# A four-block transformer on one core: query and key stripes filled straight from the rotated tiles, and the opening reordered around ten hand-placed score steps

## The chip, the cores and the metric

The kernel runs on one core of a Trainium2 chip. The metric is the device time of one execution in microseconds (us). The engines meant below are TensorE (PE, matmul; PEld its weight loads), VectorE (DVE), ScalarE (ACT), GpSimd (POOL) and SyncE (SP, which here only issues DMAs). All data are float32.

## The reference, cut to what matters

Eight sequences of 512 tokens by 256 channels pass through four residual blocks. The first block is the attention that the change is about; the other three are the same for both kernels.

```python
x = x + attn_a(layernorm(x))        # 16 heads of 16, keys and values through a latent of 64, rotary q and k
x = x + ffn(layernorm(x))           # 256 -> 1024, relu, -> 256
x = x + attn_b(layernorm(x))        # retention: (q k^T * decay) v, one head of 256
x = x + ffn(layernorm(x))

# attn_a, per sequence and head
q = x @ Wq + bq
k, v = split((x @ Wkv_down + bkv_down) @ Wkv_up + bkv_up)
q, k = rope(q), rope(k)             # [x1 cos - x2 sin, x1 sin + x2 cos]
att = softmax(q k^T / 4 + log_sparse + log(decay + 1e-9))
out = att @ v + 0.2 * sigmoid(q . mean(k)) * mean(v)
return out @ Wo + bo
```

## The kernel before, in words

**Layout.** For each sequence b (a "batch" below) the 16 heads are four groups g of four heads; a head owns 32 partitions of the tiles `qT` and `kT` ([128, 4 groups, 512]), two of each, used in turn by even and odd batches. Of a head's 32 rows, 16 hold the rotated projection, one holds minus the row maximum (in qT) against a one (in kT), and the rest are zero in qT. So one matmul over 32 rows gives scores already shifted by their maximum.

**Opening of a batch.** A layer norm (`ln_units`: statistics on DVE, `rstd` on GpSimd, `norm` on DVE, `turn` = four transposes on PE and a copy on ACT, each in two halves of the tokens), `latent` (the down projection), then `projected(j, e)`: j is 0 for queries and 1 for keys, e is the half (dimensions 0 to 7 or 8 to 15 of all 16 heads), so that the result is [128 = 16 heads x 8, 512]. `half_unit` multiplies it by the cosine and the sine table (DVE, tiles `rc` and `rs`). `turn(j)` combines the halves on GpSimd, writes them to the DRAM tensors `dk` or `dq` (two moves) and reads them back into the 32-row layout of `kT` or `qT` (four moves, one for each head of a group). `mean_k`, `gate`, `mean_v` and `through_wo` make the small memory term.

**Score steps.** A batch has 32 steps, eight to a group: four query tiles by two pairs of heads. Step t does `score_item` (s: two matmuls into PSUM), `reduce_item` (DVE, the row maximum `mr`), and for step t-10 (LAG) `prob_item` (t: the transposed, shifted scores), `soft_item` (exponential on ACT; the product with the decay table on DVE or GpSimd), and for every second step `pv_item` two steps later (PVLAG). When a group's eight maxima are there, `shift` transposes them, negates them on ACT and sends them by a DMA that ACT issues (`neg`) into the row of qT.

**Order of the work.** Every engine runs its instructions in the order in which the program writes them (`keep_in_program_order`). All moves by `move` go through SyncE's queue in that order. For the opening the order is written by hand at the end of `tile_kernel`. After that a planner takes over: it holds chains of units (`Unit`: a function, its PE time, the engines it then needs, the units before it, the first step at which it may come), and at each turn either does the next score step or takes the unit that can start first. Fillers that use PE are paid from a credit that grows with each step by the PE work left, divided by the steps left. In the kernel before, the planner's loop starts at step 0; batch 0 is then fully projected, its values, gate and the product of the retention's weights (`plain`, `product`, `product_biases`) are done, and the fillers for the first steps are batch 0's `through_wo` (from step 10) and batch 1's layer norm (from step 2) and projections.

**Names in the profile.** Line 69 is the helper that records every DVE, ACT and GpSimd operation, 205 and 208 those for matmuls and transposes, 91 that for moves; so the tile names tell operations apart: `tr_a`, `lat`, `k`, `q`, `v`, `ga`, `mv`, `me` for the opening's units, `wr`, `ct`, `bb` for plain, product and product_biases, `s` and `t` for scores, `p` for probabilities, `hx` and `x` for the two halves of the feed-forward.

Of the kernel before, what the change touches and what calls it, by code (L numbers as in the profile page):

```python
# [35 lines left out]
def tile_kernel(  # L36
# [44 lines left out]
    dr = ctx.enter_context(tc.tile_pool(name="dr", bufs=1, space=bass.MemoryType.DRAM))  # L81
# [56 lines left out]

    qT = [keep([P, NG, T], f"qT{i}") for i in range(2)]
# [7 lines left out]
    dq = [dr.tile([NH, HD, T], F32, tag=f"dq{i}", name=f"dq{i}") for i in range(2)]  # L147
    dk = [dr.tile([NH, HD, T], F32, tag=f"dk{i}", name=f"dk{i}") for i in range(2)]
# [11 lines left out]
    def buffers(i, eng):  # L160
        eng.memset(kT[i], 1.0)
        eng.memset(qT[i], 0.0)
        gps.memset(vaug[i], 1.0)

    def head_mask():
        dve.reduce_sum(hmask, ident.rearrange("p (h d) -> p h d", d=HH), axis=AX.X)
        gps.tensor_scalar(hmask, hmask, 0.5 / T, None, ALU.mult)
        gps.memset(kmean, 0.0)

    def memory_buffers():  # L170
        for i in range(2):
            gps.memset(gates[i], 0.0)
            move(gates[i][NH : NH + 1, :], rope[HD : HD + 1, 0, :])
            gps.memset(mem[i], 0.0)
        gps.memset(bo_row, 0.0)
        move(bo_row[NH : NH + 1, :], rows[D : 2 * D].unsqueeze(0))
        move(bvc, rows[0:D].rearrange("(c p) -> p c", p=P))
        gps.memset(vmean, 0.0)
        gps.memset(vmask, 0.0)
        gps.memset(vmask[:, :, NH : NH + 1], 1.0)  # L180
        for c in range(NC):
            dve.reduce_sum(
                vmask[:, c, c * HH : (c + 1) * HH], ident.rearrange("p (h d) -> p h d", d=HD), axis=AX.X
            )
        gps.tensor_scalar(bvc, bvc, 0.1, None, ALU.mult)

    late = {}

    def late_loads():
        late["dec_a"] = resident(decay_a, "dec_a")  # L190
        xs[1] = load_x(1)

        for g in range(NG):
            at_row = (g % 2) * 4 * HD
            move(wo_sb[at_row : at_row + 4 * HD, g // 2, :], wo.rearrange("(h d) g n -> h d g n", d=32)[:, :HD, g, :])
        late["w1"] = resident(w1, "w1_sb")
        late["w2"] = resident(w2, "w2_sb")

        move(wvu[:, :, :D], wb[:, :, 2, :])
        late["dec_b"] = resident(decay_b, "dec_b")  # L200
# [12 lines left out]

    wq_sb = keep([P, NC, 2, P], "wq_sb")

    wk_sb = keep([P, P], "wk_sb")
    def regroup():
        for e in range(2):
            half_of = slice(e * HH, (e + 1) * HH)
            act.copy(  # L220
                wk_sb[e * LAT : (e + 1) * LAT, :].rearrange("p (h d) -> p h d", d=HH),
                wk_in[e * LAT : (e + 1) * LAT, :, half_of],
            )
        for e in range(2):
            half_of = slice(e * HH, (e + 1) * HH)
            for c in range(NC):
                act.copy(wq_sb[:, c, e, :].rearrange("p (h d) -> p h d", d=HH), wq_in[:, c, :, half_of])
# [4 lines left out]
    def biases():  # L232
        pick = keep([P, 2, 32], "pick")
        for e in range(2):
            act.copy(
                pick[:, e, :].rearrange("p (s d) -> p s d", d=HH),
                ident.rearrange("p (s d) -> p s d", d=32)[:, :, e * HH : (e + 1) * HH],
            )
        ps = misc("qk_bias")
        for g in range(NG):  # L240
            for j, v in enumerate((V_BQ, V_BK)):
                for e in range(2):
                    mm(ps[g * 32 : g * 32 + 32, 2 * j + e : 2 * j + e + 1], pick[:, e, :], vec[:, v + g : v + g + 1])
        act.copy(qk_bias.rearrange("p j e -> p (j e)"), ps[:, :4])
# [12 lines left out]

    def plain(j):
        ps = misc(f"wr{j}")
        for o in range(NC):  # L260
            for c in range(NC):
                flip(ps[:, o * D + c * P : o * D + (c + 1) * P], wqk_in[:, c, j, o * P : (o + 1) * P])
        wr[j] = rs.tile([P, NC, D], F32, tag="xr", bufs=3, name=f"wr{j}")
        act.copy(wr[j].rearrange("p o d -> p (o d)"), ps)

    def product():
        ps = misc("ct")
        for c in range(NC):
            for o in range(NC):
                mm(ps[:, c * D : (c + 1) * D], wr[1][:, o, c * P : (c + 1) * P], wr[0][:, o, :], o == 0, o == NC - 1)  # L270
        dve.tensor_copy(ct.rearrange("p c d -> p (c d)"), ps)
# [76 lines left out]
    def front1(b):  # L348
        def latent():
            ps = misc(f"lat_{b}")  # L350
            for c in range(NC):
                mm(ps, wd_sb[:, c].rearrange("p j n -> p (j n)"), xT_a[b]["xT"][:, c, :], c == 0, c == NC - 1)
            lt = fr.tile([P, T], F32, tag="lat", name=f"lat_{b}")
            lsum[b] = fr.tile([P, 1], F32, tag="lsum", name=f"lsum_{b}")
            act.activation(lt, ps, AF.Identity, bias=vec[:, V_BD : V_BD + 1], accum_out=lsum[b])
            lat_a[b] = lt
# [19 lines left out]
        def mean_v():  # L376
            ps = misc(f"mv_{b}")
            for c in range(NC):
                mm(ps[:, c : c + 1], wv_sb[:LAT, c * P : (c + 1) * P], lsum[b][:LAT])
            m = fr.tile([P, NC], F32, tag="mv_a", name=f"mv_a_{b}")  # L380
            dve.scalar_tensor_tensor(m, ps[:, :NC], 0.1 / T, bvc, ALU.mult, ALU.add)
            for c in range(NC):
                gps.tensor_scalar(vmean[:, c, : NH + 1], vmask[:, c, :], m[:, c : c + 1], None, ALU.mult)
# [9 lines left out]
        u = {"lat": Unit(latent, 1720, (("ACT", 700),), after=[h0[2], h1[2]])}  # L393
# [8 lines left out]
    def front2(b, u1):  # L402
        rot = {}
# [17 lines left out]
        def half_unit(j, e, ps):  # L421
            for n, table in (("c", cos), ("s", nsin)):
                t = fr.tile([P, T], F32, tag="rot", bufs=6, name=f"r{n}{j}{e}_{b}")
                dve.scalar_tensor_tensor(t, ps, qk_bias[:, j, e : e + 1], table, ALU.add, ALU.mult)
                rot[n, e] = t

        def turn(j):

            d = (dq, dk)[j][b % 2]
            for e in range(2):  # L430
                o = rot["c", e]
                if e == 0:
                    gps.tensor_add(o, o, rot["s", 1])
                else:
                    gps.tensor_sub(o, o, rot["s", 0])
                move(d[:, e * HH : (e + 1) * HH, :], o)
            src = d.rearrange("(g s) r t -> s r g t", s=4)
            to = (qT, kT)[j][b % 2]
            for h in range(4):
                move(to[h * 32 : h * 32 + HD], src[h])  # L440
            if j == 0:
                if b > 1:
                    move(to[HD:P:32], zero_rows)
                rot["q"] = rot["c", 0], rot["c", 1]

        def mean_k():
            m = fr.tile([P, 2], F32, tag="mk", name=f"mk_{b}")
            for e in range(2):
                unused = fr.tile([P, T], F32, tag="unused", name=f"unused{e}_{b}")
                act.activation(unused, rot["c", e], AF.Identity, accum_out=m[:, e : e + 1])  # L450
                gps.tensor_scalar(kmean[:, e, :NH], hmask, m[:, e : e + 1], None, ALU.mult)

        def gate():
            ps = misc(f"ga_{b}")
            for e in range(2):
                mm(ps, kmean[:, e, :], rot["q"][e], e == 0, e == 1)
            act.activation(gates[b % 2][:NH, :], ps[:NH, :], AF.Tanh)
# [9 lines left out]
        ga = Unit(gate, 1720, (("ACT", 600),), after=[km, qt], needs=(("wo", b - 2),))  # L467
        return [lat] + k + [kt, km] + q + [qt, u1["v"], ga, u1["mv"], u1["me"]]
# [23 lines left out]
    def shift(i):  # L492
# [5 lines left out]
        act.dma_start(qT[b % 2][HD:P:32, g, :], neg)  # L498
# [237 lines left out]
    order0 = front2(0, front[0][1])  # L736
    (n0, n1), u0 = (front[0][0][:3], front[0][0][3:]), front[0][1]
    buffers(0, dve)
    head_mask()
    n0[0].fn(), n1[0].fn()  # L740
    biases()
    regroup()
    n0[1].fn(), n1[1].fn()
    n0[2].fn(), n1[2].fn()
    memory_buffers()
    for u in order0[:7]:
        u.fn()
    late_loads()
    plain(0), plain(1)
    for u in order0[7:10]:  # L750
        u.fn()
    product(), product_biases()
    buffers(1, gps)


# [127 lines left out]
    for u in front[0][0] + order0[:10]:  # L883
        u.done = 0
    order0[10].step = 10
    chains = [order0[10:], setup]
    for b in range(1, B):
        ln0, u1 = front1(b)
        ln0[0].step = ln0[3].step = max(0, PER * (b - 1) + 2)
# [8 lines left out]
    t, credit, share = 0, 0, 0  # L898
# [156 lines left out]
```

## Time and profile before

| | us |
|---|---|
| median of 3 timed runs | 1343.89 (1341.66 to 1344.90) |
| profiled run, its time | 1341.52 |
| profiled run, span of the core | 1339.7 |
| TensorE busy | 1256.3 (94%) |
| VectorE busy | 811.0 (61%) |
| ScalarE busy | 450.0 (34%) |
| GpSimd busy | 405.8 (30%) |
| mean granted TensorE clock | 0.978 |

Times inside the profile count from the start of the span. A line of the timeline gives the start, the duration, the engine, the line, the operation, what it writes and reads, the shapes and the count of merged instructions; in brackets stands the idle time before it and what ended that. In a row of the stages, each engine has its busy time and its number of instructions, then come the granted TensorE clock as a share of full speed, the mean busy share of the 16 DMA engines and what they moved. Where the clock has no record, as in the first 20 us, the row shows 1.00; the durations of the matmuls tell there how fast the array ran. A float32 matmul appears as two instructions.

### The profile page before, as it was taken

Reading aid. Unit: us, or ns where it says so; the run is one execution under the profiler, and the core shown is the slowest. Engines: PE = TensorE matmul, PEld = TensorE weight load, DVE = VectorE, ACT = ScalarE, POOL = GpSimd, SP = SyncE. Lnnn points to the kernel's source line nnn. Section 1 sums busy time; section 2 is a strip of 40 time slices with the busy share of each in tenths; the row PEclk is TensorE's granted clock in tenths of the full one; section 3 lists DMA queues with packets and bytes.
Section 4 is the critical chain, followed back from the end, with each engine's and each line's share of the span. In section 5 each row is a group of like instructions: output and inputs, shape, how many; then the busy total and the mean of one; then the engine's idle time right before and its main releaser. Section 6 shows DMA issues by size and latency. Waiting matters only on the chain. (4 is left out here: it accounts for less than half of the span.)

```text
span 1339.7 us, 15533 instructions
## 1 busy us (share of the span) xinstructions
PE 1256.3 (94%) x6116; PEld 623.3 (47%) x6116; DVE 811.0 (61%) x1323; ACT 450.0 (34%) x646; POOL 405.8 (30%) x461
## 2 busy tenths in 40 slices
PE   6899888999899999999999999999999899999988
PEld 3333232534354455453443554544444445455665
DVE  4588885667656774657856666657755575343130
ACT  2044434333434334433334334333333333321201
POOL 4165542324412432215332323214321232222010
PEclk9599999989899999999999999999999999998999
DMA  5440030012000210004000310003000000000000
GB/s 133 133 80 1 1 80 1 1 26 55 1 17 1 62 19 1 1 17 80 1 1 1 74 22 1 1 9 73 1 1 5 12 1 1 1 17 1 0 16 16
DMA packets 22798, 32.34 MB, mean 24 GB/s; under 512 B 3627, under 2 KB 13228, under 8 KB 22446
## 3 DMA queue, kind: packets, MB, share of 16 engines
q1 hardware_dynamic: 22086, 31.10, 10.1%
q8 instruction: 48, 0.79, 0.3%
q10 hardware_dynamic: 640, 0.26, 0.1%
q14 instruction: 24, 0.20, 0.1%
HBM read 18.50 MB, written 12.58 MB: 23 GB/s over the span
## 5 line engine op out<-in xcount | busy, mean ns | idle before, releaser
L69 DVE TENSOR_REDUCE mr<-s 128x2 f32<-128x1024 f32 x256 | 312.8, 1222 | 251.7 <-PE t L205 237.2
L69 ACT ACTIVATE p<-t 128x1024 f32<-128x1024 f32 (+1 forms) x290 | 263.8, 924 | 519.3 <-PE t L205 476.3
L69 POOL TENSOR_TENSOR p<-p,dec_a 128x512 f32<-128x512 f32 x182 | 233.1, 1301 | 507.6 <-ACT p L69 495.0
L205 PE MATMUL s<-kT,qT 32*128 32x512 f32 x1024 | 295.3, 660 | 49.3 <-DVE mr L69 44.4
L205 PE MATMUL t<-qT,kT 32*128 32x512 f32 x1024 | 294.7, 642 | 0.3 <-ACT p L69 0.3
L69 DVE TENSOR_TENSOR p<-p,dec_a 128x512 f32<-128x512 f32 x330 | 228.9, 735 | 21.0 <-ACT p L69 20.8
L205 PE MATMUL x<-w_sb,h_x 128*128 128x256 f32 x1024 | 233.9, 384 | 0.0
L205 PEld LDWEIGHTS x<-w_sb,h_x 128*128 128x128 f32 x1024 | 190.8, 190 | 54.5 <-issue 30.1
L205 PEld LDWEIGHTS s<-kT,qT 32*128 32x128 f32 x1024 | 81.2, 189 | 221.8 <-DVE mr L69 97.5
L205 PE MATMUL pv<-p,va 128*32 128x512 f32 x1024 | 151.7, 612 | 2.9 <-DVE p L69 2.4
L69 ACT ACTIVATE h_x<-hx,vec 128x512 f32<-128x512 f32 x128 | 88.0, 687 | 151.8 <-PE hx L205 151.8
L205 PE MATMUL hx<-xT_f,w_sb 128*128 128x512 f32 x256 | 120.2, 609 | 0.7 <-ACT xT_f L69 0.7
L205 PE MATMUL hx<-xT_g,w_sb 128*128 128x512 f32 x256 | 119.3, 609 | 0.7 <-ACT xT_g L69 0.7
L69 DVE TENSOR_TENSOR x<-x,x 128x256 f32<-128x256 f32 x64 | 27.1, 423 | 148.3 <-PE x L205 148.3
L205 PEld LDWEIGHTS t<-qT,kT 32*128 32x128 f32 x1024 | 80.5, 184 | 15.9 <-ACT p L69 7.8
L205 PEld LDWEIGHTS hx<-xT_g,w_sb 128*128 128x128 f32 x256 | 46.8, 193 | 63.5 <-issue 58.1
L205 PEld LDWEIGHTS hx<-xT_f,w_sb 128*128 128x128 f32 x256 | 46.5, 194 | 58.3 <-issue 51.6
L205 PEld LDWEIGHTS pv<-p,va 128*32 128x32 f32 x1024 | 23.3, 108 | 79.3 <-issue 37.0
L69 POOL TENSOR_TENSOR x<-x,row 128x256 f32<-128x256 f32 x64 | 48.0, 770 | 32.1 <-DVE xn_f L69 21.4
L69 POOL TENSOR_TENSOR rc<-rc,rs 128x512 f32<-128x512 f32 x32 | 42.3, 1342 | 5.6 <-DVE rs L69 5.6
L205 PE MATMUL bs<-xT_r,ret 128*128 128x512 f32 (+3 forms) x128 | 38.0, 442 | 0.0
L205 PE MATMUL bo<-ret 128*128 128x256 f32 x160 | 36.6, 383 | 0.0
(130 smaller groups left out, 1020.1 us busy)
## 6 DMA issues: line engine op xcount, KB each, us to landing
dk<-rc SPq DMA_DIRECT2D x16, 256.0 KB, 2.9
kT<-dk SPq DMA_DIRECT2D x32, 128.0 KB, 3.2
dq<-rc SPq DMA_DIRECT2D x16, 256.0 KB, 2.9
qT<-dq SPq DMA_DIRECT2D x32, 128.0 KB, 3.8
out_dram<-x SPq DMA_DIRECT2D x32, 128.0 KB, 1.7
x<-in_x_dram SPq DMA_DIRECT2D x7, 512.0 KB, 3.6
w_sb<-in_w_dram SPq DMA_DIRECT2D x2, 1024.0 KB, 10.1
x<-in_x_dram SPq DMA_DIRECT2D x2, 256.0 KB
```

The costliest lines, as they stand in the source:

```text
L69: ins = f(*a, **k)
L205: tc.keep_in_program_order(nc.tensor.matmul(o, lhsT=l, rhs=r, start=start, stop=stop))
```

## The change

The DRAM tensors `dq` and `dk` are gone. A rotated tile goes to qT or kT by four moves, one for each group, each from 32 neighbouring partitions (four heads by eight dimensions) to 32 partitions that lie four apart (`stripes`). A head's row order changes with it (dimension d of half e lies at row 4d + 2e, the maximum at row 1), for queries and keys alike. So a turn is eight moves in place of six.

The opening is rewritten by hand: PE first runs 14 products of the identity (`warm`); batch 0's latent is computed in two halves, each as soon as its half of the tokens is transposed; queries' first half comes before the keys; the second query half is rotated on DVE in place of GpSimd; loads that the first steps need (second x, decay table, gate rows) are issued before the stripes, and the rest after them; memsets move from DVE to GpSimd or later on DVE. The first ten score steps are then called by hand, with `plain(1)`, the two halves of `product`, the shift of group 0 and batch 0's gate between them. Batch 0's `mean_v` (from step 12), `through_wo` and `product_biases` (from step 20) become fillers, and batch 1's layer norm may start from step 10 on. The planner starts at step 10, with no credit.

```diff
-    dr = ctx.enter_context(tc.tile_pool(name="dr", bufs=1, space=bass.MemoryType.DRAM))
...
+    def loads_before_scores():
+        xs[1] = load_x(1)
+        late["dec_a"] = resident(decay_a, "dec_a")
+        for i in range(2):
+            move(gates[i][NH : NH + 1, :], rope[HD : HD + 1, 0, :])
+        move(bvc, rows[0:D].rearrange("(c p) -> p c", p=P))
...
+    def warm(n):
+        ps = misc("warm")
+        for j in range(n):
+            mm(ps[:, j % 4 * P : (j % 4 + 1) * P], ident, ident)
...
-        def latent():
-            ps = misc(f"lat_{b}")
+        def latent(part=0, parts=1):
...
+            ps = misc(f"lat_{b}_{part}")
+            n = T // parts
+            cols = slice(part * n, (part + 1) * n)
...
+        def rotate(j, e, eng):
+            o = rot["c", j, e]
+            if e == 0:
+                eng.tensor_add(o, o, rot["s", j, 1])
+            else:
+                eng.tensor_sub(o, o, rot["s", j, 0])
+            rot[j, e] = o
+
+        def stripes(j, g, e):
+            move((qT, kT)[j][b % 2][2 * e : P : 4, g, :], rot[j, e][g * 32 : g * 32 + 32, :])
 
         def turn(j):
-
-            d = (dq, dk)[j][b % 2]
             for e in range(2):
-                o = rot["c", e]
-                if e == 0:
-                    gps.tensor_add(o, o, rot["s", 1])
-                else:
-                    gps.tensor_sub(o, o, rot["s", 0])
-                move(d[:, e * HH : (e + 1) * HH, :], o)
-            src = d.rearrange("(g s) r t -> s r g t", s=4)
-            to = (qT, kT)[j][b % 2]
-            for h in range(4):
-                move(to[h * 32 : h * 32 + HD], src[h])
-            if j == 0:
-                if b > 1:
-                    move(to[HD:P:32], zero_rows)
-                rot["q"] = rot["c", 0], rot["c", 1]
+                rotate(j, e, gps)
+                for g in range(NG):
+                    stripes(j, g, e)
+            if j == 0 and b > 1:
+                move(qT[b % 2][1:P:32], zero_rows)
...
-        act.dma_start(qT[b % 2][HD:P:32, g, :], neg)
+        act.dma_start(qT[b % 2][1:P:32, g, :], neg)
...
-    buffers(0, dve)
-    head_mask()
+    dve.memset(kT[0], 1.0)
+    gps.memset(vaug[0], 1.0)
+    memory_buffers()
+    picks()
+    warm(14)
+    regroup_k()
     n0[0].fn(), n1[0].fn()
+    n0[1].fn(), n1[1].fn()
+    n0[2].fn()
     biases()
-    regroup()
-    n0[1].fn(), n1[1].fn()
-    n0[2].fn(), n1[2].fn()
-    memory_buffers()
-    for u in order0[:7]:
-        u.fn()
+    regroup_q(0)
+    latent(0, 2)
+    masks()
+    dve.memset(qT[0], 0.0)
+    gps.memset(kT[1], 1.0)
+    gps.memset(qT[1], 0.0)
+    gps.memset(vaug[1], 1.0)
+    loads_before_scores()
+    n1[2].fn()
+    latent(1, 2)
+    regroup_q(1)
+    half_unit(0, 0, projected(0, 0))
+    k_ps = [projected(1, e) for e in range(2)]
+    half_unit(1, 0, k_ps[0]), half_unit(1, 1, k_ps[1], "sc")
+    rotate(1, 0, gps), rotate(1, 1, gps)
+    half_unit(0, 1, projected(0, 1), "sc")
+    rotate(0, 1, dve), rotate(0, 0, dve)
+
+    for g in range(NG):
+        for j, e in ((1, 0), (1, 1), (0, 1), (0, 0)):
+            stripes(j, g, e)
     late_loads()
-    plain(0), plain(1)
-    for u in order0[7:10]:
-        u.fn()
-    product(), product_biases()
-    buffers(1, gps)
+    order0[1].fn()
+    plain(0)
+    gps.tensor_scalar(bvc, bvc, 0.1, None, ALU.mult)
+    order0[0].fn()
...
+    ga0.after = []
+    mv0.step = 12
+    chains = [[mv0, me0, Unit(product_biases, 2400, (("DVE", 500),), step=20)], setup]
     for b in range(1, B):
         ln0, u1 = front1(b)
-        ln0[0].step = ln0[3].step = max(0, PER * (b - 1) + 2)
+        ln0[0].step = ln0[3].step = max(LAG, PER * (b - 1) + 2)
...
+    between = {
+        1: Unit(lambda: plain(1), 700, (("ACT", 600),)),
+        3: Unit(lambda: product(0), 900),
+        5: Unit(lambda: product(1), 900, (("ACT", 600),)),
+        9: ga0,
+    }
+    for t in range(LAG):
+        step(t)
+        if t in between:
+            issue(between[t])
+        if t == 8:
+            issue(posts.pop(0))
+
+    t, credit, share = LAG, 0, 0
```

In this cut `order0[1]` is batch 0's `values` and `order0[0]` its `mean_k`. A helper `spare` gives the second query half of batch 0 a tile of the probabilities' pool, the plain weights `wr` lie in the tile of `x1`, and the product's copy out of PSUM moves from DVE to ACT.

## The prediction

> **What bounds the kernel now.** I read the page first (busy times and the forty slices), then a table of stages, then the opening in order of time, then the steps after it, and last SyncE's waits and the DMA issues. The page:
>
> ```profile
> span 1339.7 us, 15533 instructions
> PE 1256.3 (94%) x6116; PEld 623.3 (47%) x6116; DVE 811.0 (61%) x1323; ACT 450.0 (34%) x646; POOL 405.8 (30%) x461
> PE   6899888999899999999999999999999899999988
> PEclk9599999989899999999999999999999999998999
> ```
>
> TensorE is the bound from the fourth slice on, and the change leaves that long part as it is: after the opening both kernels have the same matmuls to do. What can be won lies in the first two slices, where PE is at 6 and then "busy" at half clock. The stages of that opening:
>
> ```profile
> core 0: us, PE busy (x) PEld busy (x) DVE busy (x) ACT busy (x) POOL busy (x), PEclk, DMA share, GB/s
> 33.40:38.00 4.60, 0.00 (x0) 0.00 (x1) 1.48 (x2) 0.00 (x0) 1.49 (x2) 0.54 0.53 96
> 38.00:52.00 14.00, 13.96 (x29) 4.66 (x30) 8.71 (x13) 0.00 (x0) 0.95 (x2) 0.50 0.96 277
> 52.00:64.00 12.00, 10.35 (x33) 4.76 (x33) 6.69 (x11) 1.44 (x3) 0.95 (x2) 0.62 0.03 12
> 64.00:100.00 36.00, 33.07 (x166) 11.57 (x165) 29.15 (x35) 15.29 (x31) 21.37 (x19) 1.00 0.38 73
> 100.00:127.00 27.00, 26.99 (x155) 8.91 (x148) 21.43 (x28) 13.67 (x27) 16.03 (x13) 1.00 0.01 2
> ```
>
> For 4.6 us PE has nothing; then ten score steps run at clock 0.50. The timeline says what PE waited for:
>
> ```profile
> 11.88 3.78 PE L205 MATMUL lat<-xT_a,wd_sb 128*128 128x512 f32 x4 [0.92 <-ACT xT_a L69]
> 16.53 2.08 PE L205 MATMUL k<-lat,wk_sb 64*128 64x512 f32 x4 [0.87 <-ACT lat L69]
> 22.75 1.79 SPq L91 DMA_DIRECT2D dk<-rc  x2
> 27.07 1.74 SPq L91 DMA_DIRECT2D kT<-dk  x4
> 28.91 2.52 SPq L91 DMA_DIRECT2D dq<-rc  x2
> 34.74 1.72 SPq L91 DMA_DIRECT2D qT<-dq  x4
> 38.00 13.91 PE L205 MATMUL s<-kT,qT 32*128 32x512 f32 x28 [4.64 <-DMA qT<-dq]
> 63.98 0.70 PE L205 MATMUL s<-kT,qT 32*128 32x512 f32 x2
> 63.99 0.70 PE L205 MATMUL t<-qT,kT 32*128 32x512 f32 x2
> ```
>
> The reader sees the keys leave at 22.75, come back from DRAM, the queries queue behind them on SyncE, and the first score at 38.00. Step 10 (the first with a probability, t) begins at 63.98. Two spans thus carry everything: 38.0 us to the first score, 26.0 us for ten steps. The sum below is made against the profiled run, 1341.5 us; the median of the timed runs, 1343.9, is 2.4 above it, and I carry the difference over to that. About 0.3%, 4 us, is what a measurement of this kernel can tell from no change.
>
> **Part 1, up to the first score.** Removed: DRAM legs, 12 moves per batch. Added: 16 stripes of 64 KB, straight from the rotated tiles. Of the way from 22.75 to 38.00 only one issue and one landing is left. SyncE issues such a move in 0.42 to 0.45 us (four kT in 1.74); landing is bounded by these rows:
>
> ```profile
> kT<-dk SPq DMA_DIRECT2D x32, 128.0 KB, 3.2
> out_dram<-x SPq DMA_DIRECT2D x32, 128.0 KB, 1.7
> ```
>
> I take 2.2, nearer the lower, as a stripe has half the bytes; no row shows a copy inside SBUF. Only the first four stripes (group 0) stand before step 0; the other twelve, 5.3 us of issue, pass while the steps run, group 1 being wanted at step 8. The moves now put in front of them (second x, decay table, gate rows, bvc) add 960 KB; the old loads end near 14 us, and at the 277 GB/s of 38 to 52 us these take 3.5 us more, so they are through before the first stripe.
>
> The chain before the stripes, step by step. The memset of qT[0] leaves the front of VectorE: statistics can start when the first half of x is in (its semaphore fills at 3.54) instead of 5.18. GpSimd first has 2.7 us more of memsets (those seen from 8.22 to 10.7), free near 5.0, so the normalised halves are ready near 6.9 and 7.9 (before: 8.0 and 10.0). PE gets fourteen warming products of 128 columns, 28 passes; at the cold rate of lat (four passes of 512 columns in 3.78) that is some 6.6 us from 1.3, so the first flips start near 7.9, no later than before. From there the parts are: flips 1.1 and ACT copy 0.6; bias products 1.3; half latent 0.9 to 1.9; second flips and copy 1.1 to 1.7; half latent 0.9 to 1.9; query half 1.8 to 3.8; both key halves 1.0 to 2.1 (warm: 1.92 at 65.05 for the same four beside other work). That puts the keys in PSUM between 16.5 and 20. VectorE has then three products of 0.66 each to the one that the first rotation needs (2.0), GpSimd two rotations of 1.27 (2.5); beside them VectorE finishes the second query half and its own two rotations of 0.74. Fourth stripe issued 5 us behind the keys, landed 2.2 later: first score at 23.5 to 28.5. I take **26**, past the middle, since lat and k ran at half rate until 20.3 in the trace even after six microseconds of work. Gain 12.0 (9.5 to 14.5).
>
> **Part 2, the ten steps.** VectorE's reduction takes 1.23, so a step cannot take less than 1.25. At clock 0.50 a step's two heads take PE 2.0 us (fourteen matmul pairs in 13.91). Between them are now: flips of plain (1.05 cold, as tr_a at 51.84; 0.45 warm), two products (me, the same four passes, took 2.08 cold; 0.9 warm in ct's 1.99 for eight), the shift's flip 0.4, gate (3.8 cold by lat, 1.7 warm). Gone from this stretch: two tr_a, lat of batch 1, me. All cold: 20+1.05+4.2+0.4+3.8 = 29.5. All warm: 12.5 for the reductions, of PE's fillers only gate and a little stand out, 15.5. PE idles some 5 us before step 0 (values and plain(0) fill under 2 of them), as it did from 33.4, so it starts cold; the products are full-array work like me and lat at 58 to 64, behind which the clock came back at 61. I take half the steps cold, 16.3, plus 0.75+3.0+0.4+2.0: **22.5**. Gain 3.5 (10.5 to a loss of 3.5).
>
> By the Trainium skill (TensorE: Matmul & The Clock Gate, Part 1), one busy window of about 3.4 us releases the clock, so the steps would be warm from the third on and the stretch near 17. The row 38 to 52 speaks against it: PE 13.96 of 14 busy and still 0.50; matmuls on 32 of 128 rows did not count as enough there. My sum goes by the row.
>
> **Part 3, what is only moved.** Done before 63.98 until now, and after step 10 from now on: statistics and norm of batch 1 (VectorE 5.2), its flips 1.1, lat 1.9, and mv, me, biases of the product (PE 0.3+0.9+2.5). PE 6.7 in all. What hides it? In steps 20 to 33 nothing is inserted and two steps take 4.65:
>
> ```profile
> 101.64 1.23 DVE L69 TENSOR_REDUCE mr<-s 128x2 f32<-128x1024 f32 x1 [0.70 <-PE t L205]
> 103.46 2.97 POOL L69 TENSOR_TENSOR p<-p,dec_a 128x512 f32<-128x512 f32 x2 [1.64 <-ACT p L69]
> 106.29 1.23 DVE L69 TENSOR_REDUCE mr<-s 128x2 f32<-128x1024 f32 x1 [1.08 <-PE t L205]
> ```
>
> That is the way round t, exponential, GpSimd's product, pv; PE has some slack in it. But steps 10 to 19 took 33.9 for 8.2 of inserted PE work, 10.6 above that pace, so inserts are paid at about 1.3 there. Bounds: 2 (all in the slack) to 9 (at 1.3); I take **6.5**. Credit for fillers also starts at nothing at step 10, and batch 1 must be projected by step 32; its pieces cost PE 15 us against 20 steps of about 3 us of credit each, so it is in time.
>
> **Part 4, batches 1 to 7.** Sixteen issues for twelve: SyncE is idle nearly always, 0. No score waits for a stripe: batch 2's keys went out at 169 and are needed at step 64, at 239. The second query half reuses tiles that four stripes, not one move, must have read; that move landed in 2.9, four take 1.7+2.2, covered by the distance from 66 to 82 us between the two in batch 1; without that cover 1 us a batch. VectorE, GpSimd: same operations. Taken as 0, from -2 to the price of the second rival. By the skill (DMA: Bandwidth & Descriptors, Rules for kernel authors) small moves should be merged, for under 64 KB they are mostly overhead; by it the sixteen would be the worse choice. The rows price it at 0.43 of an idle queue each, which is nothing.
>
> Sum: -12.0 -3.5 +6.5 = -9.0: 1332.5 as the profiled run, **1335** as a median (own range 1328 to 1340).
>
> **Rivals.** *The clock stays up* (0.20): warming and the shorter gap hold the clock, first score 24, steps 16.5, so step 10 at 40.5 instead of 64.0, moved work 5: -18.5, 1325. For it: me and lat turned the clock at 61. Against: the gap before step 0 is as long as the one at 33.4. *All of it cold* (0.17): 28 and 29.5 make step 10 at 57.5, a gain of 6.5, moved work 8: 1345, no difference. For it: the row at 0.50. *ACT stands behind the stripes* (0.18), the slower side:
>
> ```profile
> SPq L91 <- DMA rope_sb<-in_rope_dram: 2.2, 1, 2.2
> ```
>
> The move that waited (a gate row) has nothing to do with rope_sb; that load is the eighth DMA before it. So a DMA waits for the eighth before it to land. A turn used to be six moves and is now eight: the next shift's row maximum, sent from ACT's queue, then stands behind a stripe that waits for GpSimd's rotation, and all exponentials queue behind it, and PE behind those. Price: up to two products (5.0), a rotation 1.27, issue and landing 5: some 11 us of ACT for a turn that falls badly. Fourteen turns; it eats the gain at an average of 0.65 a turn and is over 4 us slower from 0.95; at 1.5 the time is 1356. Against: shifts come eight steps (some 37 us) apart, so most turns are landed long before, and ACT is 34% busy. That the stripes, being interleaved rows of one tile, would wait for each other I leave out: the move of zero rows into qT, interleaved too, was issued 0.03 us behind its neighbours.
>
> **How the numbers follow.** The forecast has 0.45. Faster by over 0.3%: most of it and the first rival, 0.64. Within: the cold rival and little else, 0.17. Slower: 0.19. The range takes the first rival's side down to 1322 and the unknown costs up to 1348.
>
> **What would show it.** Right: first s near 26 behind a DMA of qT or kT; step 10's t near 48.5; clock 0.50 for part of the steps only; products of bb beyond step 20; the end earlier by 6 to 12. Wrong: first s after 30; the ten steps over 29; ACT's neg issue preceded by idle time that a stripe ends; or the distance from step 10 to the end grown by over 9.

## The result, and the profile after

The changed kernel takes the same time as the one before: a median of 1343.45 us over twelve runs (1339.20 to 1346.04) against 1342.05 for before on the same chip, a ratio of 1.0011 with a 95% interval of 0.9993 to 1.0030. The forecast was 9 us faster, 1335; the measured time lies outside the forecast's own range (1328 to 1340) and inside the wide one (1322 to 1348). The profiled run of the changed kernel took 1346.04 us (span 1344.3), the slowest of its twelve; that of before 1341.52 (1339.7). So the two traces differ by 4.6 us and the medians by 1.4: part of what the traces show belongs to this one execution, whose mean clock of 0.970 is the lowest of the twelve (they average 0.974).

The page of the changed kernel, with the busy times, PE's slices and its clock. A record of a DMA, a matmul or a transpose now stands under line 90, 200 or 203:

```profile
span 1344.3 us, 15699 instructions
PE 1262.7 (94%) x6152; PEld 628.0 (47%) x6152; DVE 808.9 (60%) x1324; ACT 451.8 (34%) x649; POOL 402.1 (30%) x459
PE   6999888989899999999999999999999899999988
PEclk8779989989899999999999999999999999998999
```

PE is at 9 in the second to fourth slices (8, 9 and 9 before), and its clock there is 0.7, 0.7 and 0.9 (0.5, 0.9 and 0.9 before): faster in the second, slower in the third. The stages answer to those shown of before:

```profile
24.50:30.90 6.40, 2.90 (x18) 1.45 (x16) 5.41 (x10) 1.93 (x5) 3.74 (x5) 1.00 0.19 49
30.90:51.90 21.00, 18.59 (x61) 7.12 (x61) 13.98 (x15) 2.03 (x4) 0.94 (x2) 0.76 0.59 198
51.90:130.30 78.40, 75.08 (x352) 28.65 (x353) 52.84 (x75) 30.63 (x60) 38.16 (x36) 0.83 0.06 15
130.30:1344.30 1214.00, 1149.98 (x5640) 580.16 (x5638) 726.26 (x1205) 411.75 (x565) 348.61 (x392) 0.98 0.04 12
```

The bounds of these rows are the first score, step 10 and the reduction of step 32. Cut at the same steps, the kernel before has:

```profile
64.00:127.20 63.20, 60.26 (x313) 20.49 (x313) 50.78 (x62) 29.16 (x58) 37.59 (x31) 1.00 0.22 43
127.20:1339.70 1212.50, 1148.78 (x5640) 580.66 (x5638) 727.09 (x1205) 411.52 (x565) 348.62 (x392) 0.99 0.08 17
```

Against the sum of the prediction:

| term | predicted, us | between the two traces, us |
|---|---|---|
| Part 1, first score (38.0 to 30.9) | -12.0 | -7.1 |
| Part 2, ten steps (26.0 to 21.0) | -3.5 | -5.0 |
| Part 3, step 10 to step 32 (63.2 to 78.4) | +6.5 | +15.2 |
| Part 4, step 32 to the end (1212.5 to 1214.0) | 0 | +1.5 |
| sum | -9.0 | +4.6 |

Followed step by step, the reductions of the changed kernel are 8.8 us early at step 0, 10.9 at step 12, 9.0 at step 20, 3.9 at step 24, and 3.1 late from step 28 on. The gain is there for twenty steps and is gone eight steps later.

Two things are to be explained: why the first score came at 30.9 and not at 26, and where the 15.2 us went. For the first, the timeline of ACT and PE:

```profile
7.93 1.13 PE L200 MATMUL lat<-xT_a,wd_sb 128*128 128x256 f32 x4
9.19 0.61 SPq L90 DMA_DIRECT2D vec<-in_vecs_dram  x1
14.82 0.47 ACT L69 ACTIVATE lat<-lat,vec 128x256 f32<-128x256 f32 x1 [4.63 <-DMA vec<-in_vecs_dram]
15.28 0.57 ACT L69 COPY xT_a<-tr_a 128x512 f32<-128x512 f32 x1
15.91 2.08 PE L200 MATMUL lat<-xT_a,wd_sb 128*128 128x256 f32 x4 [6.41 <-ACT xT_a L69]
```

The first half of the latent left PE near 9, but its bias for rows 64 to 127 comes by a second small move into `vec` (64 rows of 4 bytes), the fifteenth in SyncE's order. It was issued at 9.19 and ACT could go on at 14.82. The copy of the second transposed half is queued behind the latent on ACT, so PE stood still for 6.41 us. In the kernel before, the same move was issued at the same time, but ACT reached the latent only at 15.70, because PE's latent ended only then, and the move was hidden:

```profile
9.21 0.61 SPq L91 DMA_DIRECT2D vec<-in_vecs_dram  x1
15.70 0.69 ACT L69 ACTIVATE lat<-lat,vec 128x512 f32<-128x512 f32 x1 [3.87 <-PE lat L205]
```

For the second, each matmul's time up to the start of the next one, summed by tile between step 10 and step 32 in both traces, gives 63.4 and 78.5 us. Of the difference of 15.1, work that was not there before takes about 10.5: `bb` 3.6, `tr_a` 2.2, `lat` 1.9, `mv` 1.9, `me` 1.0. The rest, 4.6, is the old work going slower. Of this stretch 27.3 us ran at clock 0.50, in three spans (52.2 to 62.4, 82.9 to 96.6, 110.2 to 113.6); before, none did. PE's busy time grew by 14.8 of the 15.2: there was no slack to take anything in.

### The profile page after: what moved, and what is told of

It is laid out like the page before. It is cut to its first block, busy times and chain, and to the rows that moved or that the text cites. A ratio compares the mean times of both kernels' runs of the same rounds, so it can differ in the third digit from the quotient of the medians.

```text
span 1344.3 us, 15699 instructions
## 1 busy us (share of the span) xinstructions
PE 1262.7 (94%) x6152; PEld 628.0 (47%) x6152; DVE 808.9 (60%) x1324; ACT 451.8 (34%) x649; POOL 402.1 (30%) x459
## 5 line engine op out<-in xcount | busy, mean ns | idle before, releaser
L200 PE MATMUL t<-qT,kT 32*128 32x512 f32 x1024 | 301.7, 658 | 2.0 <-DMA qT<-neg 1.7
L69 POOL TENSOR_TENSOR rc<-rc,rs 128x512 f32<-128x512 f32 x30 | 39.4, 1335 | 12.4 <-DVE rs L69 12.4
```

The costliest lines, as they stand in the source:

```text
L69: ins = f(*a, **k)
L200: tc.keep_in_program_order(nc.tensor.matmul(o, lhsT=l, rhs=r, start=start, stop=stop))
```

## The experiments

Where not said otherwise a kernel is the changed one with one edit. Ratios are to the kernel before, with 95% intervals.

**The stripes alone.** The kernel before, with the DRAM tensors replaced by stripes and nothing reordered:

```diff
...
-                move(d[:, e * HH : (e + 1) * HH, :], o)
-            src = d.rearrange("(g s) r t -> s r g t", s=4)
-            to = (qT, kT)[j][b % 2]
-            for h in range(4):
-                move(to[h * 32 : h * 32 + HD], src[h])
+                for g in range(NG):
+                    move(to[2 * e : P : 4, g, :], o[g * 32 : g * 32 + 32, :])
...
-        act.dma_start(qT[b % 2][HD:P:32, g, :], neg)
+        act.dma_start(qT[b % 2][1:P:32, g, :], neg)
```

> The kernel before with the stripes alone: opening order, planner and all else as before. The stripes theory (sixteen moves a batch cost something in batches 1 to 7): no gain or a loss, distance from step 10 to the end longer than before's by several us. The two others (clock; moved work): the batches do not feel it, distance from step 32 to the end unchanged within 1.5 us; the first score comes when PE has done the product's biases, near 33.5 instead of 38.0, and the end comes 3 to 6 us earlier.

Measured 1337.03 us, 0.9963 (0.9950 to 0.9976). This part alone is a gain. Its timeline and stages:

```profile
22.37 4.99 SPq L90 DMA_DIRECT2D kT<-rc  x8
27.46 6.22 SPq L90 DMA_DIRECT2D qT<-rc  x8
34.20 1.14 PE L202 MATMUL s<-kT,qT 32*128 32x512 f32 x8
34.20:56.50 22.30, 17.82 (x62) 6.68 (x61) 16.15 (x25) 1.44 (x3) 3.51 (x6) 0.69 0.53 177
56.50:119.70 63.20, 60.26 (x313) 20.44 (x313) 50.81 (x63) 29.19 (x58) 37.68 (x31) 1.00 0.10 26
```

The first score is 3.8 us earlier although all sixteen stripes stand in front of it, and PE no longer waits for it: there is no bracket behind it, as the last bias product ends at 34.27. From step 10 to 32 the stretch is that of before, 63.2, and from there to the end it is 1212.1 against 1212.5. So the stripes cost the seven later batches nothing that shows, and the third rival, ACT behind the stripes, falls. What the whole change lost lies in its other parts.

**PE kept warm.** Four products of the identity ahead of the scores of steps 10 to 31, into the PSUM bank that the scores then overwrite:

```diff
+            ps_s = ps
...
+        if s is not None and 10 <= t < 32:
+            for _ in range(4):
+                mm(ps_s[:, 0, :P], ident, ident)
```

> The changed kernel with four more products of the identity (128 columns, 8 passes, 0.43 us at full clock) put ahead of the score matmuls of each of steps 10 to 31, 9.4 us of PE work that nothing needs. Clock theory (the gain of the opening is lost because steps 10 to 32 run a third of their time at half clock): the clock stays at 1.00 from about step 13 on, step 10 to step 32 takes some 68 to 72 us instead of 78, the end comes 3 to 8 us earlier although PE does more. Moved-work theory (the stretch is longer by the work moved into it, the clock is a by-product): 4 to 9 us slower.

Measured 1349.73 us, 1.0046 (1.0034 to 1.0058).

```profile
51.70:136.40 84.70, 82.61 (x524) 43.49 (x521) 53.74 (x75) 30.28 (x60) 37.65 (x36) 0.96 0.05 14
```

The clock is 0.96 instead of 0.83, with 6.8 us at half rate instead of 27.3, and the stretch is 6.3 us longer all the same: to buy the clock with such work does not pay. How the 15.2 divide between the clock and the moved work, this run does not settle. The 88 products took 23.4 us from one start to the next, where 9.4 had been expected, too much for it: the clock alone would make 63.2 + 23.4 = 86.6 at full rate, near the 84.7 measured, but moved work beside a clock effect and gaps that took up part of the products would make the same.

**The bias products moved into the hand steps**, behind step 7:

```diff
-    chains = [[mv0, me0, Unit(product_biases, 2400, (("DVE", 500),), step=20)], setup]
+    chains = [[mv0, me0], setup]
...
+        7: Unit(product_biases, 2400, (("DVE", 500),)),
```

> The changed kernel with product_biases (20 products of one column, 2.9 us) back among the ten hand-placed steps, behind step 7, instead of being a filler from step 20 on. Clock theory: the stretch of one-column products at step 20 was what let the clock fall for 13.7 us, that cold stretch is gone, end 3 to 7 us earlier. Moved-work theory: only its own 2.9 us change place into a stretch where VectorE is the bound, 0 to 3 us earlier.

Measured 1342.41 us, 0.9996 (0.9985 to 1.0007). Step 10 came at 53.4 instead of 51.9, and the stretch to step 32 took 73.1 instead of 78.4, with 15.4 us at half clock instead of 27.3. Of these 5.3 us 3.6 are the products themselves; what they then cost in front, and 0.2 later, leaves the profiled run 3.6 faster, the median 1.0, which cannot be told from none.

**The weights' loads written at step 14**, to clear the DMA engines for the first row maximum:

```diff
+    def weights():
         move(wvu[:, :, :D], wb[:, :, 2, :])
         late["w1"] = resident(w1, "w1_sb")
...
+    setup = [Unit(weights, step=14), Unit(lambda: fetch(2), step=20)]
```

> The changed kernel with the 2.5 MB of feed-forward and retention weights issued from step 14 on, not right behind the stripes, so that group 0's row maximum (sent at 46.5, 5.4 us on its way) does not share the DMA engines with them. Both theories: it lands in under 2.5 us and step 10's t starts 2 to 3 us after the gate's matmuls at most. Clock theory: the half-clock stretch behind that wait goes too, end 3 to 6 us earlier. Moved-work theory: 2 to 3 us earlier, no more than the wait.

Measured 1341.69 us, 0.9990 (0.9974 to 1.0007): no difference that can be told. ACT sent the row maximum at 46.89 (46.54 in the changed kernel), and step 10 began at 52.6 (51.9).

```profile
41.09 1.07 SPq L90 DMA_DIRECT2D w_sb<-in_w_dram  x2
46.89:52.60 5.71, 3.70 (x13) 1.01 (x9) 3.98 (x7) 0.59 (x1) 0.94 (x2) 1.00 0.68 258
```

But the edit did not delay the loads. SyncE runs ahead of the other engines, nothing in its own queue held the moves back, and it issued the large weights at 41.09, as in the changed kernel (41.27). While the row maximum was on its way the DMA engines still moved 258 GB/s (306 in the changed kernel, from 46.54 to 51.94). So this run does not tell whether the large loads are what the wait is made of; that stays open.

**The moved work put back** among the hand steps: batch 1's norm and latent, `mv`, `me` and the bias products, so that from step 10 on PE has the order of the kernel before.

```diff
-    mv0.step = 12
+    chains = [[mv0, me0, Unit(product_biases, 2400, (("DVE", 500),))], setup]
...
+        for c in {0: (2,), 1: (2,), 2: (2, 2), 3: (2,), 4: (2,), 6: (2, 0), 7: (0,), 8: (0,)}.get(t, ()):
+            issue(chains[c].pop(0))
```

> The changed kernel with all that the change moved behind step 10 put back among the ten hand-placed steps (batch 1's layer norm and latent, mean_v, through_wo, product_biases); behind step 10 the order of PE's work is then that of the kernel before. Moved-work theory (each microsecond of PE work put into steps 10 to 32 lengthens them by about one, and a fallen clock adds about a quarter of its time): step 10's t comes 5 to 9 us later than in the changed kernel, near 57 to 61; step 10 to step 32 falls from 78 back to 63 to 65; the end is 3 to 8 us earlier than the changed kernel's. Stripes theory: the 78 stay.

Measured 1344.67 us, 1.0023 (1.0007 to 1.0040).

```profile
30.70:66.30 35.60, 34.02 (x102) 14.24 (x102) 16.06 (x27) 3.39 (x7) 2.71 (x7) 0.64 0.29 103
66.30:130.10 63.80, 61.11 (x313) 20.88 (x313) 50.84 (x63) 29.04 (x57) 37.73 (x31) 0.99 0.09 26
```

The stretch from step 10 is back at 63.8 (63.2 before), and the ten steps take 35.6. The sum is 99.4, to the tenth that of the changed kernel (21.0 + 78.4), though 25.4 us at half rate now lie in the first row and 1.6 in the second (10.2 and 27.3 in the changed kernel). Set-up that PE must do between the first score and step 32 costs its time at either place: this is what the first score's 7.1 us were paid with. The half-rate time fell from 37.5 to 27.0 us without making the sum smaller, so what the clock takes of it stays open.

**The planner from step 0**, with the changed opening: all set-up of PE ahead of the first score, no steps by hand. And the same with the second move into `vec` directly behind the first.

```diff
-    plain(0)
+    plain(0), plain(1)
...
-    order0[0].fn()
+    order0[0].fn(), order0[2].fn(), order0[3].fn()
+    product(0), product(1), product_biases()
...
-    for t in range(LAG):
-        step(t)
...
-    t, credit, share = LAG, 0, 0
+    t, credit, share = 0, 0, 0
```

> The changed kernel's opening and stripes alone: no hand-placed steps; values, plain, gate, mean_v, product and its biases run on PE before the first score as they did, and the planner starts at step 0. Moved-work theory: step 10 to step 32 is 63 to 64 as before, first score near 35 (PE's work ends there, not the stripes), end near that of the kernel before with stripes alone, 1335 to 1340. If instead the reordered opening itself (not the placing of the steps) is what lost the gain, it stays near 1343.

> As a7_planner, and the small move that fills the second half of the latent's bias column (64 rows of 4 bytes) is issued right behind the first move of vec, not as the fifteenth. In the changed kernel ACT waited 4.6 us for it at 14.8, with the latent and the second half of the transposed tokens behind that wait. Expected: latent's ACT at 10 to 11 in place of 14.8, first score 4 to 6 us earlier than in a7_planner, end 4 to 6 us earlier. A rival says that the next late load (wk, wq or the tables) takes its place and less than 2 us come of it.

Without the early move 1339.48 us, 0.9979 (0.9965 to 0.9994); with it 1336.11, 0.9944 (0.9922 to 0.9965). In the first the stretch from step 10 to 32 is 63.0 and the first score is at 39.2, five later than with the old opening and stripes, for PE's set-up waits behind the late latent:

```profile
39.20:64.60 25.40, 22.04 (x62) 8.26 (x61) 15.67 (x25) 1.44 (x3) 1.90 (x4) 0.53 0.31 115
64.60:127.60 63.00, 60.32 (x313) 20.70 (x313) 50.78 (x62) 29.16 (x58) 37.63 (x31) 1.00 0.10 26
```

In medians the hand-placed steps are 4.0 slower than the planner (1343.45 against 1339.48). The reordered opening is 2.4 slower than the old one (1339.48 against 1337.03), but the intervals of the two overlap (0.9965 to 0.9994 and 0.9950 to 0.9976), so that this difference is not shown.

**The early move in the changed kernel.**

```diff
     vec = resident(vecs, "vec")
+    move(vec[LAT:, V_BD : V_BD + 1], vecs[:LAT, V_BD : V_BD + 1])
...
-    move(vec[LAT:, V_BD : V_BD + 1], vecs[:LAT, V_BD : V_BD + 1])
```

> The changed kernel with that same small move early, and nothing else. Expected: first score at 25 to 27 in place of 30.9, as the prediction had it; what is won before step 10 is kept to the end, as the order behind it does not change: 3 to 5 us earlier than the changed kernel, unless the clock's phase takes some of it.

Measured 1339.65 us, 0.9972 (0.9960 to 0.9984), but the first score is at 29.8, only 1.1 earlier:

```profile
1.73 3.38 SPq L90 DMA_DIRECT2D vec<-in_vecs_dram  x2
7.76 0.60 SPq L90 DMA_DIRECT2D wq_in<-in_wq_dram  x1
13.82 0.49 ACT L69 COPY wq_sb<-wq_in 128x128 f32<-128x128 f32 x2 [2.44 <-DMA wq_in<-in_wq_dram]
14.22 0.47 ACT L69 ACTIVATE lat<-lat,vec 128x256 f32<-128x256 f32 x1
```

The second move writes the column that the first has just written, so SyncE stood until that had landed, and every load behind it went out up to 2.9 us later (`wq_in` at 7.76 instead of 4.88). ACT then waited for `wq_in` instead. The edit was right and its place wrong.

**The same move behind `wq_in`**, where the first has long landed: in the changed kernel, and in the version with the planner.

```diff
     move(wq_in.rearrange("p c h d -> p c (h d)"), wq[:, :, 0, :])
+    move(vec[LAT:, V_BD : V_BD + 1], vecs[:LAT, V_BD : V_BD + 1])
...
-    move(vec[LAT:, V_BD : V_BD + 1], vecs[:LAT, V_BD : V_BD + 1])
```

> The changed kernel, with the small load of the latent's bias (64 rows of 4 bytes) issued right behind wq_in, where the load ahead of it has already landed, so that SyncE does not stop for it as it did for 2.9 us when the move stood one place behind the first vec. Theory (the first score failed to reach 26 because ACT's latent waited 4.63 us for this load, and what the first score gains is worth little as long as the PE work behind it is the same): latent on ACT near 10 to 11 in place of 14.82, first score 26 to 27.5 in place of 30.9, step 10 near 47 to 49; of these 4 us about 3 to 4 reach the end, since here idle time of PE is removed and no work is moved: 4 us faster than the changed kernel, 0.996 to 0.998 of the kernel before. Rival (another late load takes the place, as wq_in did in the run with the early move): first score 29 or later and the same time as that run, 0.997 or above.

> The opening of the changed kernel with all of PE's set-up ahead of the first score and the planner from step 0 (no steps by hand), and the same small load behind wq_in. Theory: first score 34.5 to 36 in place of 39.2 without the move and 38.4 with it one place behind the first vec; step 10 near 60; later stages as in those two; time 2 to 4 us below the 1336.1 of the latter, 0.992 of the kernel before, the fastest of all. Rival (wq_in was no obstacle, and the stop of SyncE cost nothing): same as 0.9944.

1338.24 us, 0.9953 (0.9938 to 0.9968), and 1332.72 us, 0.9930 (0.9909 to 0.9951). In the changed kernel:

```profile
5.61 0.54 SPq L90 DMA_DIRECT2D vec<-in_vecs_dram  x1
11.51 0.50 ACT L69 COPY wq_sb<-wq_in 128x128 f32<-128x128 f32 x2 [3.41 <-DMA wq_in<-in_wq_dram]
11.91 0.47 ACT L69 ACTIVATE lat<-lat,vec 128x256 f32<-128x256 f32 x1
27.94 2.09 PE L200 MATMUL s<-kT,qT 32*128 32x512 f32 x8 [3.29 <-DMA qT<-rc]
27.90:49.60 21.70, 19.38 (x61) 7.25 (x61) 13.99 (x15) 2.03 (x4) 0.94 (x2) 0.73 0.57 192
49.60:128.20 78.60, 74.44 (x352) 28.35 (x353) 54.15 (x75) 30.55 (x60) 38.95 (x36) 0.85 0.06 15
```

The first score is 3.0 earlier than in the changed kernel (30.9), and the median is 5.2 lower. Both rows behind it are as before the edit, 21.7 and 78.6. Here idle time of PE was removed and no work was moved, so the gain stays. With the planner in place of the hand steps:

```profile
34.60:55.80 21.20, 17.85 (x62) 6.69 (x61) 15.48 (x25) 1.44 (x3) 1.91 (x4) 0.68 0.39 144
55.80:118.70 62.90, 60.22 (x313) 20.64 (x313) 50.76 (x62) 29.14 (x58) 37.65 (x31) 1.00 0.10 26
```

Its first score comes 6.7 us after that of the hand-placed version, and its step 32 comes 9.5 us before. By its median this is the fastest kernel of the study, 5.5 us below the hand-placed version with the same move and 4.3 below the stripes alone; its interval still overlaps those of these two and of the planner with the early move (0.9922 to 0.9965).

**The latent ahead of the query weights on ACT**, in that fastest version, to tell whether the latent now waits for `wq_in` or for its bias:

```diff
-    regroup_q(0)
     latent(0, 2)
...
     n1[2].fn()
+    regroup_q(0)
```

> The fastest version so far (the opening of the changed kernel with its small load behind wq_in, and the planner from step 0), with ACT's two copies of the first query weights moved from ahead of the latent's first half to behind the copy of the second transposed half. It tells which load the latent waits for now: the profile named wq_in for 3.36 us. Theory (it is wq_in, and only because ACT keeps order): latent on ACT near 9 to 10 in place of 11.86, the query product then waits for wq_in; first score 33 to 34.5 in place of 34.6 and the time 0 to 2 us below 1332.7, 0.992 of the kernel before. Rival (the bias load itself lands only then): latent still near 11.5 to 12, nothing gained, and the weights' copies now come 1 us later: first score 35 or later, 0.993 to 0.994.

1335.90 us, 0.9949 (0.9930 to 0.9968); the interval overlaps that of the version above (0.9909 to 0.9951), so the two cannot be told apart.

```profile
11.13 0.47 ACT L69 ACTIVATE lat<-lat,vec 128x256 f32<-128x256 f32 x1 [3.04 <-DMA vec<-in_vecs_dram]
32.80:58.20 25.40, 22.04 (x59) 8.25 (x60) 15.67 (x25) 1.44 (x3) 1.90 (x4) 0.54 0.31 115
```

It was the bias itself: the latent moved forward by 0.7 only and waits for `vec` again, 5.5 us after its issue. The first score is 1.8 earlier (32.8 against 34.6), as the early halves now ran at full rate, and yet step 10 is 2.4 later (58.2 against 55.8): the ten steps ran 23.2 us at half clock instead of 13.7. An earlier first score is once more not an earlier end.

## Why the prediction was wrong, point by point

**Part 1** failed in the step of the loads. It said that the old loads end near 14 us and are through before the first stripe, and it built the chain from what stands before each piece on the compute engines alone. That ACT's latent needs one of the last of those loads was not looked for: ACT was ready 4.63 us before 14.82, and the load held it. Of the 4.9 us that Part 1 fell short, moving this load won back 3.0. The rest of that chain was sound. With the move behind `wq_in` the first score is at 27.9, inside its bounds of 23.5 to 28.5; the keys are in PSUM at 19.8 (16.5 to 20 were given); and the fourth stripe is issued at 25.78, 6.0 behind them (5 was taken), with the score 2.16 after that (2.2 was taken). The issue of one stripe took 0.54 to 0.60 rather than 0.42 to 0.45.

**Part 2** was right, 21.0 for 22.5, with about ten of its 21 us at half clock, where half the steps had been taken as cold.

**Part 3** was mis-sized, 15.2 for 6.5 and over its upper bound of 9. Two things failed. The lower figure rested on slack on PE between steps 20 and 33; the row of before shows PE busy 60.26 of 63.2, the prediction's own row from 100 to 127 even 26.99 of 27.0, and nearly all of the growth is busy time. And the moved work was priced at a full clock that it then upset: its 6.7 of PE work took 10.5, the old work beside it 4.6 more, and 27.3 us ran at 0.50. At full rate the moved work would take 7.3 (`bb` 2.2, `lat` 1.9, `tr_a` 1.2, `mv` 1.0 for its two halves, `me` 1.0), so that about half of the 15.1 is moved work and half is clock, an estimate that no single run shows. The text had costed cold and warm for the ten steps, but not for the stretch behind them.

By the Trainium skill (TensorE: Matmul & The Clock Gate, Part 1) the clock falls after a window of about 3.4 us in which PE was idle. The fall at 31.7 agrees: PE had been idle for 3.31 us before the first score. Two rows do not: the clock fell at 82.9 behind scores and bias products that kept PE busy for 3.2 of the 3.4 us before, and in the kernel before it fell at 33.8, only 0.4 us after PE had stopped. Why it falls there was not tested.

**Part 4** was right: the same 5640 matmul records from step 32 on, and no wait of SyncE for a stripe. The 1.5 us that remain go with a longer half-rate span (168.2 to 175.1 against 166.9 to 170.3) and an additional one (212.6 to 216.0).

**The rivals.** *The clock stays up* did not happen: 0.76 in the ten steps and 0.83 behind them. *All of it cold* named nearly the right time, 1345, by luck, on the wrong terms: its first score at 28 and ten steps at 29.5 were both off (30.9 and 21.0), and what cancelled the gain was Part 3. *ACT stands behind the stripes* fell by the kernel with stripes alone. The rule against small moves, which the text had weighed by the Trainium skill (DMA: Bandwidth & Descriptors, Rules for kernel authors; a stripe, with 64 KB, lies just at its limit), did not decide either: sixteen small moves with one landing were faster than twelve moves with two landings in a row.

**What would show it.** The signs named for wrong were the ones that came: first score after 30, and the distance from step 10 to the end grown by more than 9 (by 16.7: 1292.4 against 1275.7).

**The clock from run to run.** Over the twelve runs of the changed kernel the time falls by 7 us for each 0.01 of mean granted clock, over the 68 runs of before by 11 us. The changed kernel's mean is 0.974 and that of before 0.978. If the two are related as those slopes say, 3 to 4 us of the missing gain are clock. All the kernels with hand-placed steps and no added products average 0.974 to 0.975, the versions with the planner or the old opening 0.977 to 0.980.

**What adds up, in medians.** They come from different chips, on which the kernel before took 1342.0 to 1343.9, so differences of 2 us or so are not shown. Stripes about -5 (1337.03); the reordered opening +2.4 (1339.48) as long as one small load comes late, and about -4 against the stripes alone where it does not (1332.72); the hand-placed steps +4.0 where that load comes late (1343.45) and +5.5 where it does not (1338.24 against 1332.72). What the hand-placed steps cost is moved work and clock, in shares that no run separates.

## What to carry to other kernels

On an engine that is busy all the time, an earlier start of the main loop is worth only the idle time that it removes: list what was hidden in the old wait, and price it at full cost, cold clock included, where it goes. When a chain is shortened, check for each of its pieces every load that it reads, small ones too, for what was hidden behind the old chain ends last next; and try the parts of a large change one by one, for here one of three carried a gain and another paid it back. When an edit is to delay a load, look in the trace whether it did.

## What was not expected of the hardware

A load of 64 rows of 4 bytes took 5.5 to 5.6 us from issue to its reader at both places where the reader was waiting (9.19 to 14.82, 5.61 to 11.13), while a 64 KB stripe between two tiles took 2.2. The DMA engines moved 301 and 227 GB/s during the two small loads and were busy for nearly all of the time (share 1.08 and 0.90); during the stripe that the first score waited for (28.72 to 30.88) it was 110 GB/s and 0.42. That the large loads beside it held the small one is likely by these numbers, but no run tests it. The Trainium skill (DMA: Bandwidth & Descriptors, Anatomy of one DMA — SWDGE (gpsimd) path) gives about 2.0 us as the fixed part of a transfer that GpSimd issues. These moves were issued by SyncE, so the figure is only a neighbour's: the stripe's 2.2 is close to it, the small load's 5.5 is not.

The first ten score steps with nothing of PE's set-up ahead of them left (62 records of matmuls in the same order) took 21.2 us in the fastest version, with 13.7 us at half clock, and 25.4, with 24 at half clock, in the planner version that differs from it only in where the small load stands. So some 0.4 us were lost for each microsecond at half rate; the traces show no difference in the work of the two, only that it began at another time. The ratio is not a rule: with the moved work put back, 10.5 us less at half rate left the same 99.4 us.
